# Cross-attention over 25,088 keys: stationary columns interleaved in memory, and value products of odd key tiles walked from the last column to the first

## The chip, the core and the metric

The kernel runs on one core of one Trainium2 chip. The time is device microseconds of one execution of the whole program. The kernel before takes 586.98 us (median of two runs, 586.13 and 587.82). The execution that the profiler recorded took 586.28 us.

## What is computed

One block of a perceiver: 256 latent rows `x` of width 512 attend to a context of 25,088 rows, then a causal self-attention with 16 heads and a mixture of eight small experts follow. Nearly all of the time goes into the first step, which is this part of the reference (`q` is the layer-normed `x`, `k` and `v` are the context; there is no softmax, the weights are sigmoids):

```python
qp = jnp.einsum('bsd,ed->bse', q, Wq) + bq
kp = jnp.einsum('bsd,ed->bse', k, Wk) + bk
vp = jnp.einsum('bsd,ed->bse', v, Wv) + bv
z = jnp.einsum('bqe,bke->bqk', qp, kp)
z = jax.nn.sigmoid(z / scale)
return jnp.einsum('bqk,bkd->bqd', z, vp)
```

Here `d` is 512 and `e` is 128. The kernel multiplies the sigmoids with the raw context and applies `Wv` once at the end, and adds the bias by the row sums of the sigmoids.

## The kernel before, in words

The context is cut into 49 chunks of 512 keys, and each chunk into four key tiles of 128. It comes twice, transposed (`ctxT`, for the key projection) and plain (`ctxN`, for the value product).

Every matmul operand is held as two float32r tensors, a high half that ScalarE writes (`copy`, L64) and a low half, the remainder, that VectorE writes (L65). A product is then three matmuls, high x high, high x low, low x high, in `mm3` (L67 to L70). In a matmul the stationary operand (`lhsT`, 128 columns) is loaded into the array first, and the moving operand (`rhs`) then streams past it; each moving column gives one output column in PSUM.

Per chunk `c` of the loop (L263 and on), the engines get:

- `kp_mm(c + 1)`, the key projection: stationary `wk` (four blocks of 128 columns, high and low in two tiles of 512), moving `T`, 512 columns: 4 x 3 matmuls into the bank `kp_ps`. `kp_out` adds the bias (ScalarE L178, VectorE L179) and makes `kp`.
- `av(c, t, q)`, the value product, for key tile `t` (0 to 3) and half `q` (0 or 1) of the 256 latent rows: stationary `z`, the 128 sigmoids of that tile and half, moving `N`, the 512 context columns, accumulated over the whole loop into `acc0` and `acc1`: 8 x 3 matmuls.
- `scores(c + 1, p)` for the pairs of key tiles `p` = 0 (tiles 0 and 1) and `p` = 1 (tiles 2 and 3): stationary `kp`, moving `qp`, 256 columns: 2 x 2 x 3 matmuls into `sc`. The sigmoid (ScalarE L187) gives `z` in float32, VectorE adds it to the running row sums `zacc` (L189), and `split` makes the high and low tiles of the pair, 512 columns each: columns of tile 0 and then of tile 1, and within a tile rows 0 to 127 and then 128 to 255.
- the splits of the next chunks' `T` and `N` (2048 columns each), and, spread over the loop, the preparing of later weights (`prepare`).

`z` has four buffers for each half and pair, `T`'s high half and `N` have two, `T`'s low half has one. In the last two chunks `av` runs for `q` = 0 alone, and the rest is used later as filler (`AV1`). `in_order` keeps each engine's instructions in the order in which the program was written; Tile adds the semaphores. All loads are issued from SP's queue in the order of the code.

Before the loop, `wk` is loaded and split once, the high half by ScalarE, the low half by GpSimd. At the end, in the experts, the tiles `fr` and `fq` (the gated products) lie where `wk`'s two tiles were.

Of the kernel before, what the change touches and what calls it, by code (L numbers as in the profile page):

```python
# [11 lines left out]
F32 = mybir.dt.float32  # L12
F32R = mybir.dt.float32r
# [7 lines left out]
P = 128  # L21
T = 256
D = 512
KD = D // P
# [3 lines left out]
NT = CK // P  # L28
E = 8
NH = 16  # L30
LAG = 2
# [17 lines left out]
def body(ctx, tc, a, out, nch=NCH):  # L49
    nc = tc.nc  # L50
# [4 lines left out]
    sb = ctx.enter_context(tc.tile_pool(name="sb", bufs=1))  # L55
# [3 lines left out]
    def f(t):  # L59
        return t.bitcast(F32)  # L60

    def split(hi, lo, src, eng=nc.vector):

        copy(hi, src)  # L64
        eng.tensor_tensor(lo, src, f(hi), ALU.subtract)  # L65

    def mm3(ps, ahi, alo, bhi, blo, first, last):  # L67
        mm(ps, lhsT=ahi, rhs=bhi, start=first, stop=False)  # L68
        mm(ps, lhsT=ahi, rhs=blo, start=False, stop=False)  # L69
        mm(ps, lhsT=alo, rhs=bhi, start=False, stop=last)  # L70

    def pair(name, shape, tag=None, bufs=1):
        return [sb.tile(shape, F32R, tag=f"{tag or name}{i}", name=f"{name}_{i}", bufs=bufs) for i in range(2)]

    def bank(name):
        return psum.tile([P, D], F32, tag="b", name=name, bufs=6)
# [4 lines left out]
    def toks(t):  # L81
        return slice(t * P, (t + 1) * P)
# [39 lines left out]
    def moments(x, tag):  # L122
        s6 = sm.tile([P, nc.vector.BN_STATS_DIM], F32, tag="s6", name=f"s6{tag}", bufs=2)
        mv = sm.tile([P, 2], F32, tag="mv", name=f"mv{tag}", bufs=2)
        rs = sm.tile([P, 1], F32, tag="rs", name=f"rs{tag}", bufs=2)
        nc.vector.bn_stats(s6, x)
        nc.vector.bn_aggr(mv, s6)
        nc.vector.tensor_scalar(rs, mv[:, 1:2], 1e-5, None, ALU.add)
        nc.gpsimd.tensor_tensor(rs, rs, half, ALU.pow)
        return mv, rs  # L130
# [12 lines left out]
    rT, rN, sT, sN, kp, zz = {}, {}, {}, {}, {}, {}  # L143
# [24 lines left out]
    def kp_mm(c, blocks=range(KD)):  # L168
        th, tl = sT[c]
        if c not in kp:  # L170
            kp[c] = bank(f"kp_ps{c}")
        ps = kp[c]
        for j in blocks:
            mm3(ps, wk[0][:, toks(j)], wk[1][:, toks(j)], th[:, j, :], tl[:, j, :], j == 0, j == KD - 1)

    def kp_out(c):
        ps, kp[c] = kp[c], pair(f"kp{c}", [P, CK], "kp", 2)
# [3 lines left out]
    def scores(c, p):  # L181
        ps = bank(f"sc{c}_{p}").rearrange("p (i t) -> p i t", i=2)
        for i in range(2):
            t = toks(2 * p + i)
            mm3(ps[:, i, :], kp[c][0][:, t], kp[c][1][:, t], qp[0], qp[1], True, True)
        z = sb.tile([P, 2, T], F32, tag="z", name=f"z{c}_{p}", bufs=2)
        nc.scalar.activation(z, ps, AF.Sigmoid, scale=1.0 / math.sqrt(128.0))  # L187
        zz[c, p] = pair(f"z{c}_{p}", [P, 2, T], "z", 2 * LAG)
        tt2(zacc, zacc, z, ALU.add)  # L189
        split(*zz[c, p], z)  # L190

    def av(c, t, q):
        zh, zl = zz[c, t // 2]
        nh, nl = sN[c]
        mm3(acc[q], zh[:, t % 2, toks(q)], zl[:, t % 2, toks(q)], nh[:, t, :], nl[:, t, :],
            c == 0 and t == 0, c == nch - 1 and t == NT - 1)

    def prepare(n):

# [12 lines left out]
    def load_split(n, tag):  # L212
        r = sb.tile([P, D], F32, tag="wr", name=f"{n}_r", bufs=2)
        nc.sync.dma_start(r, a[n])
        return r, pair(n, [P, D], tag)

    wk_r, wk = load_split("wk", "wk")
    for t in range(2):
        nc.sync.dma_start(x_sb[t], a["x"][:, t, :])
    wq_r, wq = load_split("wq", "at")  # L220
# [9 lines left out]
    acc = [psum.tile([P, D], F32, tag=f"acc{q}", name=f"acc{q}") for q in range(2)]  # L230
    xh, xl = pair("xa", [P, KD, T], "oh")
    warm = sm.tile([P, 1], F32, name="warm")
    nc.scalar.activation(warm, half, AF.Sigmoid)
    split(*wk, wk_r, nc.gpsimd)
    m = [moments(x_sb[tt], f"a{tt}") for tt in range(2)]
    xn = [normal(x_sb[tt], m[tt], f"xa{tt}") for tt in range(2)]
    split(*wq, wq_r, nc.gpsimd)
# [1 line left out]
    for j in range(2):  # L239
        split_T(0, [j])  # L240
        split(xh[:, :, toks(j)], xl[:, :, toks(j)], xps[j])
    split_T(0, [2, 3], nc.gpsimd)
    kp_mm(0, [0, 1])
    qp = pair("qp", [P, T])
    ps = bank("qp_ps")[:, :T]
    for j in range(KD):
        mm3(ps, wq[0][:, toks(j)], wq[1][:, toks(j)], xh[:, j, :], xl[:, j, :], j == 0, j == KD - 1)
    kp_mm(0, [2, 3])
    split_T(1, [0, 1])
    split_T(1, [2, 3], nc.gpsimd)  # L250
    nc.scalar.activation(qp[0], ps, AF.Identity, bias=bq)
    nc.vector.scalar_tensor_tensor(qp[1], ps, bq, f(qp[0]), ALU.add, ALU.subtract)
    kp_out(0)
    split_N(0, [0, 1])
    kp_mm(1, [0, 1])
    scores(0, 0)
    scores(0, 1)
    split_N(0, [2, 3])
    kp_mm(1, [2, 3])
# [3 lines left out]
    for c in range(nch):  # L263
# [23 lines left out]
        for t in range(NT):  # L287
            for q in now:
                av(c, t, q)
            if nx and t in (1, 2):  # L290
                scores(c + 1, t - 1)
# [265 lines left out]
    def AV1(n):  # L557
        for _ in range(min(n, len(late))):
            av(*late.pop(0), 1)
# [5 lines left out]
    ps = bank("rows_ps")  # L565
# [54 lines left out]
    Q(1, 2)  # L620
    Q(1, 3)
    ft = sb.tile([P, 2 * D], F32R, tag="wq2", name="ft").rearrange("p (n b e d) -> p n b e d", n=2, b=2, e=2)
    fr, fq = (sb.tile([P, 2, 2, P], F32, tag=f"wk{i}", name=f"f{i}") for i in range(2))
    yhl = pair("y", [P, KD, T], "oh")
    PV(0, 2)
    PV(0, 3)
# [144 lines left out]
```

## Time and profile before

| what | value |
|---|---|
| the profiled execution's time | 586.28 us |
| its span | 584.5 us |
| TensorE matmul, busy | 570.6 us, 98% |
| stationary loads, busy | 481.7 us, 82% |
| VectorE, busy | 459.7 us, 79% |
| ScalarE, busy | 395.1 us, 68% |
| value-product matmuls (`acc`) | 3 x 392, about 392 ns each in the record |
| key-projection matmuls (`kp_ps`) | 3 x 196 made (4 are missing in the trace), about 391 ns each |
| score matmuls (`sc`) | 3 x 196, about 283 ns each |
| z splits on VectorE | 98, 686 ns each |
| z casts on ScalarE | 98, 623 ns each |

A matmul's record covers its whole way through the array, so neighbouring records overlap: matmuls of 512 columns start about 0.227 us apart in the loop although each lasts 0.39. The granted TensorE clock is full over the span. Times in the timeline are microseconds from the span's start; what stands in brackets at the end of a line is the idle time before that instruction and what ended it.

### The profile page before, as it was taken

How to read it: one execution, taken by the hardware profiler on the slowest of the kernel's cores; microseconds unless marked ns; L12 is line 12 of the kernel's file. 1: busy time of each engine (PE TensorE's matmuls, PEld its weight loads, DVE VectorE, ACT ScalarE, POOL GpSimd, SP SyncE). 2: the span in 40 equal slices, each digit the busy share in tenths (PEclk: the TensorE clock that was granted, in tenths of full speed). 3: DMA queues.
4: the chain of work that ended last, by engine and by line, in shares of the span. 5: the costliest groups of instructions: out<-in, count | busy, mean ns of one | idle time of the engine just before them, and what ended most of it. 6: DMA issues, size and time to landing. Idle time of an engine off the chain costs nothing.

```text
span 584.5 us, 8061 instructions
## 1 busy us (share of the span) xinstructions
PE 570.6 (98%) x3036; PEld 481.7 (82%) x3036; DVE 459.7 (79%) x528; ACT 395.1 (68%) x512; POOL 21.1 (4%) x28
## 2 busy tenths in 40 slices
PE   4999999999999999999999999999999999999997
PEld 3888888888888888888888888888888887876996
DVE  6898888888888888888888888787878765667543
ACT  5877777777777777777777776767676752574211
POOL 5200000000000000000000000000000041000000
PEclk9999999999999999999999999999999999999999
DMA  8897887879888888788988887565657477700000
GB/s 288 334 368 283 278 295 281 321 278 317 287 324 276 325 271 325 266 337 298 332 282 319 274 337 245 208 225 206 234 198 243 149 295 262 316 1 1 1 1 36
DMA packets 33526, 144.94 MB, mean 248 GB/s; under 512 B 4240, under 2 KB 4432, under 8 KB 19792
## 3 DMA queue, kind: packets, MB, share of 16 engines
q1 hardware_dynamic: 33488, 144.44, 69.3%
q8 instruction: 23, 0.38, 0.2%
q14 instruction: 15, 0.12, 0.1%
HBM read 129.22 MB, written 15.20 MB: 247 GB/s over the span
## 4 chain that ended last, share of the span: by engine, by line
PE 95%; DVE 3%; DMA 1%; issue 0%; POOL 0%; ACT 0%; SPq 0%; POOLq 0%
PE acc L68 15%; PE acc L69 15%; PE acc L70 15%; PE kp_ps L70 8%; PE kp_ps L69 8%; PE kp_ps L68 8%; PE sc L70 4%; PE sc L69 4%; PE sc L68 4%; PE s L428 2%; PE gu L68 1%; PE gu L69 1%; PE gu L70 1%; PE pt L445 1%; DMA wq_r<-in_wq 1%; PE pv L456 1%
## 5 line engine op out<-in xcount | busy, mean ns | idle before, releaser
L68 PE MATMUL acc<-N,z 128*128 128x512 f32 x392 | 153.9, 393 | 0.0
L69 PE MATMUL acc<-N,z 128*128 128x512 f32 x392 | 153.7, 392 | 0.0
L65 DVE TENSOR_TENSOR N<-rN,N 128x2048 fp32r<-128x2048 f32 (+1 forms) x53 | 111.6, 2110 | 52.3 <-ACT N L64 52.2
L70 PE MATMUL acc<-N,z 128*128 128x512 f32 x392 | 152.5, 389 | 0.0
L65 DVE TENSOR_TENSOR T<-rT,T 128x2048 fp32r<-128x2048 f32 (+1 forms) x49 | 110.3, 2252 | 15.3 <-ACT T L64 15.3
L187 ACT ACTIVATE z<-sc 128x512 f32<-128x512 f32 x98 | 58.7, 599 | 66.5 <-PE sc L70 66.2
L64 ACT CAST N<-rN 128x2048 fp32r<-128x2048 f32 (+1 forms) x55 | 94.4, 1725 | 6.1
L64 ACT CAST T<-rT 128x2048 fp32r<-128x2048 f32 (+1 forms) x55 | 94.3, 1721 | 0.9 <-DMA rT<-in_ctxT 0.7
L70 PEld LDWEIGHTS acc<-N,z 128*128 128x128 f32 x392 | 73.6, 188 | 16.0
L68 PEld LDWEIGHTS acc<-N,z 128*128 128x128 f32 x392 | 74.0, 189 | 12.3
L69 PEld LDWEIGHTS acc<-N,z 128*128 128x128 f32 x392 | 74.0, 189 | 11.7
L68 PE MATMUL kp_ps<-T,wk 128*128 128x512 f32 x196 | 76.9, 392 | 0.0
L70 PE MATMUL kp_ps<-T,wk 128*128 128x512 f32 x196 | 76.7, 392 | 0.0
L69 PE MATMUL kp_ps<-T,wk 128*128 128x512 f32 x192 | 74.7, 389 | 0.0
L189 DVE TENSOR_TENSOR zacc<-zacc,z 128x512 f32<-128x512 f32 x98 | 67.2, 686 | 3.7 <-ACT z L187 1.7
L65 DVE TENSOR_TENSOR z<-z,z 128x512 fp32r<-128x512 f32 x98 | 67.3, 686 | 0.0
L64 ACT CAST z<-z 128x512 fp32r<-128x512 f32 x98 | 61.0, 623 | 3.1
L178 ACT ACTIVATE kp<-kp_ps,bk 128x512 fp32r<-128x512 f32 x49 | 33.9, 691 | 39.9 <-PE kp_ps L70 39.9
L70 PE MATMUL sc<-qp,kp 128*128 128x256 f32 x196 | 55.8, 285 | 0.1
L69 PE MATMUL sc<-qp,kp 128*128 128x256 f32 x196 | 55.4, 283 | 0.0
L68 PE MATMUL sc<-qp,kp 128*128 128x256 f32 x196 | 54.9, 280 | 0.0
L68 PEld LDWEIGHTS kp_ps<-T,wk 128*128 128x128 f32 x196 | 37.1, 189 | 7.8
(177 smaller groups left out, 658.5 us busy)
## 6 DMA issues: line engine op xcount, KB each, us to landing
rN<-in_ctxN SPq DMA_DIRECT2D x49, 1024.0 KB, 5.7
rT<-in_ctxT SPq DMA_DIRECT2D x47, 1024.0 KB, 5.5
sp_gu<-w_gu SPq DMA_DIRECT2D x32, 256.0 KB, 4.3
gu<-sp_gu SPq DMA_DIRECT2D x8, 1024.0 KB, 6.0
r_gu<-in_gu SPq DMA_DIRECT2D x16, 256.0 KB, 5.7
sp_dn<-w_dn SPq DMA_DIRECT2D x16, 256.0 KB, 4.3
dn<-sp_dn SPq DMA_DIRECT2D x16, 256.0 KB, 6.0
r_dn<-in_dn SPq DMA_DIRECT2D x8, 256.0 KB, 6.1
```

The lines of the kernel that those rows point to most:

```text
L64: copy(hi, src)
L65: eng.tensor_tensor(lo, src, f(hi), ALU.subtract)
L68: mm(ps, lhsT=ahi, rhs=bhi, start=first, stop=False)
L69: mm(ps, lhsT=ahi, rhs=blo, start=False, stop=False)
L70: mm(ps, lhsT=alo, rhs=bhi, start=False, stop=last)
L178: nc.scalar.activation(kp[c][0], ps, AF.Identity, bias=bk)
L187: nc.scalar.activation(z, ps, AF.Sigmoid, scale=1.0 / math.sqrt(128.0))
L189: tt2(zacc, zacc, z, ALU.add)
L428: mm(p3[:, h - h0:h - h0 + 2, :], lhsT=qs[:, tt, h // 2, g, :], rhs=kbd[g // 2][:, g % 2, h:h + 2, :nk], start=tt == 1, stop=tt == 0 and h ...
L445: nc.tensor.transpose(ps[:, toks(i * (tt + 1) + kt)], pr[tt, u][:, i, toks(kt)], ident)
L456: mm(pv[tt][r, g, :], lhsT=vs[kt][:, g * P + r.start:g * P + r.stop], rhs=pt[tt, u][:, toks(i * (tt + 1) + kt)], start=kt == 0, stop=kt == tt)
```

## The change

Three things about addresses, and no arithmetic:

- `wk` is one tile `[128, 4, 128, 2]`: high and low half of a column lie side by side. A stationary block is read with a step of two words.
- The high tile of a `z` pair, and likewise the low one, is laid out anew. In pair 0 the two row halves of a key tile alternate (`q` innermost): a stationary block is read with a step of two words. In pair 1 the four blocks, two key tiles by two halves, alternate: a step of four words. ScalarE and VectorE write these tiles with such steps; the float32 `z` that they read stays as it was.
- In `av`, key tiles 1 and 3 pass `back=True`: moving operand and output are both taken from column 511 down to 0, so each output column still gets its own sum.

`kp`, `qp`, `T` and the score matmuls stay. `fr` and `fq` become two halves of one tile at `wk`'s place.

```diff
-    def mm3(ps, ahi, alo, bhi, blo, first, last):
+    def mm3(ps, ahi, alo, bhi, blo, first, last, back=False):
+        if back:
+            ps, bhi, blo = ps[:, ::-1], bhi[:, ::-1], blo[:, ::-1]
         mm(ps, lhsT=ahi, rhs=bhi, start=first, stop=False)
...
-            mm3(ps, wk[0][:, toks(j)], wk[1][:, toks(j)], th[:, j, :], tl[:, j, :], j == 0, j == KD - 1)
+            mm3(ps, wk[:, j, :, 0], wk[:, j, :, 1], th[:, j, :], tl[:, j, :], j == 0, j == KD - 1)
...
-        zz[c, p] = pair(f"z{c}_{p}", [P, 2, T], "z", 2 * LAG)
+
+        if p == 0:
+            zz[c, p] = [t.rearrange("p (i t q) -> p i q t", i=2, q=2) for t in pair(f"z{c}_{p}", [P, 2 * T], "z", 2 * LAG)]
+        else:
+            zz[c, p] = [t.rearrange("p (t i q) -> p i q t", i=2, q=2) for t in pair(f"z{c}_{p}", [P, 2 * T], "z", 2 * LAG)]
         tt2(zacc, zacc, z, ALU.add)
-        split(*zz[c, p], z)
+        split(*zz[c, p], z.rearrange("p i (q t) -> p i q t", q=2))
...
-        mm3(acc[q], zh[:, t % 2, toks(q)], zl[:, t % 2, toks(q)], nh[:, t, :], nl[:, t, :],
-            c == 0 and t == 0, c == nch - 1 and t == NT - 1)
+        mm3(acc[q], zh[:, t % 2, q], zl[:, t % 2, q], nh[:, t, :], nl[:, t, :],
+            c == 0 and t == 0, c == nch - 1 and t == NT - 1, t % 2 == 1)
...
-    wk_r, wk = load_split("wk", "wk")
+    wk_r = sb.tile([P, D], F32, tag="wr", name="wk_r", bufs=2)
+    nc.sync.dma_start(wk_r, a["wk"])
+
+    wk = sb.tile([P, KD, P, 2], F32R, tag="wk", name="wk")
...
-    split(*wk, wk_r, nc.gpsimd)
+    split(wk[:, :, :, 0], wk[:, :, :, 1], wk_r.rearrange("p (j c) -> p j c", j=KD), nc.gpsimd)
...
-    fr, fq = (sb.tile([P, 2, 2, P], F32, tag=f"wk{i}", name=f"f{i}") for i in range(2))
+    frq = sb.tile([P, 2, 2, 2, P], F32, tag="wk", name="frq")
+    fr, fq = frq[:, 0], frq[:, 1]
```

## The prediction

> **What bounds the kernel now.** I read the page's first part, its chain and its groups, then the timeline of TensorE in three places and that of VectorE over one chunk. First the page: span and busy time, the chain by engine, and the groups that the change touches.
>
> ```profile
> span 584.5 us, 8061 instructions
> ...
> PE 570.6 (98%) x3036; PEld 481.7 (82%) x3036; DVE 459.7 (79%) x528; ACT 395.1 (68%) x512; POOL 21.1 (4%) x28
> ...
> PE 95%; DVE 3%; DMA 1%; issue 0%; POOL 0%; ACT 0%; SPq 0%; POOLq 0%
> ...
> L68 PE MATMUL acc<-N,z 128*128 128x512 f32 x392 | 153.9, 393 | 0.0
> ...
> L65 DVE TENSOR_TENSOR N<-rN,N 128x2048 fp32r<-128x2048 f32 (+1 forms) x53 | 111.6, 2110 | 52.3 <-ACT N L64 52.2
> ...
> L70 PEld LDWEIGHTS acc<-N,z 128*128 128x128 f32 x392 | 73.6, 188 | 16.0
> ...
> L65 DVE TENSOR_TENSOR z<-z,z 128x512 fp32r<-128x512 f32 x98 | 67.3, 686 | 0.0
> ...
> L64 ACT CAST z<-z 128x512 fp32r<-128x512 f32 x98 | 61.0, 623 | 3.1
> ```
>
> TensorE carries 95% of the chain and has no idle time ahead of its large groups, so the end moves with the time from one matmul's start to the next. That is not the 393 ns of the row, which overlaps with its neighbours; it has to be read from starts. Timeline of TensorE in the steady loop (start, duration, engine, line, operands):
>
> ```profile
> 199.99 0.28 PE L68 MATMUL sc<-qp,kp 128*128 128x256 f32 x1
> 200.11 0.28 PE L69 MATMUL sc<-qp,kp 128*128 128x256 f32 x1
> ...
> 201.74 0.39 PE L68 MATMUL kp_ps<-T,wk 128*128 128x512 f32 x1
> ...
> 204.46 0.39 PE L68 MATMUL acc<-N,z 128*128 128x512 f32 x1
> ```
>
> Twelve key projections start between 201.74 and 204.46: 2.72 / 12 = 0.2267 us each. Score matmuls, half as wide, start 0.120 apart. The same key projections near the beginning of the run, before TensorE is at full speed:
>
> ```profile
> 11.76 0.63 PE L68 MATMUL kp_ps<-T,wk 128*128 128x512 f32 x1
> 12.19 0.63 PE L69 MATMUL kp_ps<-N,wk 128*128 128x512 f32 x1
> 12.61 0.63 PE L70 MATMUL kp_ps<-T,wk 128*128 128x512 f32 x1
> ```
>
> There they start 0.427 apart. Half of that is 0.2133, and 0.2267 is 13.3 ns more. For the 256-wide ones 0.120 is also about 13 ns more than 512 : 256 of 0.2133. So each full-speed matmul carries a fixed 13.3 ns that doesn't depend on its width; as each has one stationary load, I put it down to that load. This is the term on which the change acts.
>
> A chunk is 36 matmuls of 512 columns and 12 of 256: 36 x 0.2267 + 12 x 0.120 = 9.60 us. VectorE's timeline shows the same period and its slack:
>
> ```profile
> 300.29 2.29 DVE L65 TENSOR_TENSOR N<-rN,N 128x2048 fp32r<-128x2048 f32 x1 [1.12 <-ACT N L64]
> ...
> 304.10 2.29 DVE L65 TENSOR_TENSOR T<-rT,T 128x2048 fp32r<-128x2048 f32 x1 [0.26 <-ACT T L64]
> 306.31 0.68 DVE L189 TENSOR_TENSOR zacc<-zacc,z 128x512 f32<-128x512 f32 x1
> 306.91 0.68 DVE L65 TENSOR_TENSOR z<-z,z 128x512 fp32r<-128x512 f32 x1
> 307.51 0.68 DVE L189 TENSOR_TENSOR zacc<-zacc,z 128x512 f32<-128x512 f32 x1
> ...
> 309.93 2.29 DVE L65 TENSOR_TENSOR N<-rN,N 128x2048 fp32r<-128x2048 f32 x1 [1.13 <-ACT N L64]
> ```
>
> The period is 309.93 - 300.29 = 9.64 us, of which VectorE is idle 1.12 + 0.26 = 1.38 us.
>
> **What the Trainium skill says.** "TensorE: Matmul & The Clock Gate", Step-by-step: what each phase is for, states that moving operand and stationary load have separate read ports, so that a load takes nothing from the running matmul; the 13.3 ns above speak against "nothing" in this kernel. "SBUF — State Buffer", Specifications, gives 16-byte lines and asks for at least two hits per line for full rate: a step of two fp32 words still has two, a step of four has one. "PSUM — Partial Sum Buffer", Specifications, has 8-byte lines and says that non-contiguous patterns slow matmuls; whether a backward walk over neighbours counts as that, it doesn't say. "Vector Engine (DVE) Microarchitecture Reference", Measured stream behaviour on trn2, gives 1.05 ns per column for neighbours and 1.7 to 2.5 ns when a stream steps over words. No access of the kernel before has an inner step other than 1 word on these operands, so its trace confirms none of the last three.
>
> **The change part by part.** The order of instructions on every engine is the same, and so is the count. What moves is addresses.
>
> 1. Key projection: 49 chunks x 12 = 588 loads read wk with a step of 2 words. Unknown on the trace. Bounds per matmul: -13.3 ns (the fixed part goes) to +13.3 ns (twice as many lines, twice the fixed part). Value: 0.
> 2. Value products of the first pair of key tiles: 49 x 12 = 588 loads, step 2. The same bounds and value.
> 3. Value products of the second pair: 588 loads, step 4. From -13.3 to +40 ns (four times the lines). A load occupies at most 0.120 us, because score matmuls bring one each in that time; if one hit per line makes it twice as long, 0.240 is 13 ns over the 0.2267 that cover it, which is within the bounds. Value: 0. I take 0 in all three because the timeline has the same 0.2267 for key projections and for the first pair's value products, and 0.228 to 0.236 for those right after scores (200.35, 200.59, 200.82), whatever tiles they read; that is what a cost of the load itself would do, whatever it reads.
> 4. Backward walk in odd tiles: 49 x 2 tiles x 2 x 3 = 588 matmuls read N and write acc from the last column to the first. Neighbours stay neighbours, in both memories. From 0 to +0.200 us each (the rate of the slow stage, 0.427 in place of 0.2267). Value: 0.
> 5. VectorE's z splits: two per chunk, 0.60 us from start to start (306.91 to 307.51), now with an input and the output at step 2 or 4. By the skill's prices, estimate: 512 x (1.7 to 2.5) + the 0.06 that 0.60 has over 512 x 1.05 = 0.93 to 1.34 us, so 0.33 to 0.74 more each, 0.66 to 1.48 per chunk. The cover is the 1.38 us of idle time; the high end passes it by 0.1 us x 48 chunks = 5 us. Late next would be the N split behind it, then kp's low half, on which the third score matmul waits. Value: 0.
> 6. ScalarE's z casts write with the same steps; no row prices it. Doubling them (+0.62 each) fits in the waits of the z and kp activations for TensorE, 66.2 + 39.9 us over 49 chunks, or 2.2 per chunk, though the N cast then starts later and eats of point 5's cover. A gain is worth nothing here. Value: 0.
> 7. wk's split happens once: ScalarE 0.62 us and GpSimd 1.26 us, ending near 5.3 us, long before the first key projection at 10.3 us. Only the GpSimd operation of the layer norm that follows at 5.34 could be pushed; x's second half isn't there until 6.03, so half a microsecond is covered. Value +0.3 us at most. The shared tile of the gated products at the end keeps its addresses and waits.
>
> Sum: 586.3 (the profiled execution: span 584.5 and 1.8 around it) + 0.3 = 586.6 us. The median of the runs is 0.7 above that execution, so 587.3 us.
>
> **The rivals.**
>
> - *More lines per load cost more (slower).* The place is the 13.3 ns. For: it is there only at full speed, as if two streams contended for memory, and 13.3 ns for 32 lines of 512 bytes would be one short beat a line. Against: "separate ports". If each of 1764 loads pays it twice: 1764 x 13.3 ns = +23.5 us, 610 us. If it goes by lines: 1176 x 13.3 + 588 x 40 ns = 15.6 + 23.5 = +39.1 us, 626 us. I take 611. It decides from 11.7 us on, 6.7 ns per load.
> - *The backward walk is slow.* For: the PSUM page. Against: the pairs stay pairs. In full, 588 x 0.200 = +118 us, 705 us; with half of it 646. I take 700.
> - *The fixed part shrinks (faster).* If load and stream contend because both climb at a fixed pace from equally aligned tiles, other steps or directions could part them. In full, 1764 x 13.3 = -23.5 us: 563 us. Half of it: 575. Nothing in the trace shows it, but nothing excludes it.
> - *VectorE becomes the bound.* From 0.69 us more per z split on. At 3 ns per column (prices that add): (1.60 - 1.29) x 2 x 48 = +30 us, 617; nearer the threshold 594. I take 600.
>
> **How the numbers follow.** Unchanged 0.32 (own range 584 to 592), more lines 0.24, shrinking 0.25, backward slow 0.14, VectorE 0.05. 2% of 587 is 11.7 us, about what a measurement of this kernel can tell from no change, so the marks are 575 and 599. Faster: half of the shrinking case, 0.13. Slower: 0.21 of more lines, 0.13 of backward, 0.03 of VectorE: 0.37. Within 2%: 0.50. The range 568 to 640 leaves out about 0.07 below and 0.11 above.
>
> **What would show it.** Right: starts of kp_ps and acc matmuls 0.2267 apart in all four key tiles, chunks of 9.64 us, z splits longer on VectorE and its idle time shorter. If kp_ps is at 0.240 and the second pair near 0.267, lines count; if tiles 1 and 3 differ from 0 and 2, it is the walk; at 0.213 to 0.220 the contention went; if kp's low half or N's split releases TensorE with its starts unchanged, it is VectorE.

## The result, and the profile after

The changed kernel takes 609.0 us (median of two runs, 608.47 and 609.52), the kernel before 586.98 us: a ratio of 1.0375, 95% interval 1.030 to 1.045. It is slower by 22 us. That lies inside the stated range (568 to 640), but not where the likeliest case put it (587.3); it is near the size that the first rival gave (611).

The page of the kernel after, the same parts as those shown of before:

```profile
span 607.5 us, 8061 instructions
...
PE 592.3 (97%) x3036; PEld 523.6 (86%) x3036; DVE 486.1 (80%) x528; ACT 415.2 (68%) x512; POOL 21.6 (4%) x28
...
PE 94%; DVE 3%; ACT 1%; POOL 1%; issue 0%; DMA 0%; POOLq 0%
...
L70 PE MATMUL acc<-N,z 128*128 128x512 f32 x392 | 167.1, 426 | 0.0
...
L71 PE MATMUL acc<-N,z 128*128 128x512 f32 x392 | 155.4, 397 | 0.0
...
L72 PEld LDWEIGHTS acc<-N,z 128*128 128x128 f32 x392 | 99.1, 253 | 8.3 <-DVE z L65 0.6
...
L65 DVE TENSOR_TENSOR z<-z,z 128x512 fp32r<-128x512 f32 x98 | 89.5, 913 | 21.5 <-ACT z L64 21.5
...
L64 ACT CAST z<-z 128x512 fp32r<-128x512 f32 x98 | 89.7, 915 | 3.1
```

TensorE still makes up the chain and still has next to no idle time ahead of the value products. Their loads waited for `z` once in the whole run, 0.6 us in the last chunk (the L72 line), so in the loop's steady chunks nothing new releases TensorE. But the records of the stationary loads for `acc` went from 188 to 253 ns in the mean, which mixes the loads of step 2 and of step 4. And of the three matmul lines the first grew by 33 ns (393 to 426), the other two by 5 to 8 (L71 to 397). One line out of three means that a place in the sequence is hit, besides something small that all share. The timeline of TensorE and its loads before, where a block of scores ends and value products begin:

```profile
200.24 0.19 PEld L68 LDWEIGHTS acc<-N,z 128*128 128x128 f32 x1
...
200.35 0.40 PE L68 MATMUL acc<-N,z 128*128 128x512 f32 x1
200.35 0.19 PEld L69 LDWEIGHTS acc<-N,z 128*128 128x128 f32 x1
...
200.59 0.40 PE L69 MATMUL acc<-N,z 128*128 128x512 f32 x1
```

Each load starts together with a matmul and belongs to the next one. The same place after, then the end of the last key tile's value products and the key projections:

```profile
199.50 0.28 PE L72 MATMUL sc<-qp,kp 128*128 128x256 f32 x1
199.50 0.31 PEld L70 LDWEIGHTS acc<-N,z 128*128 128x128 f32 x1
199.62 0.51 PE L70 MATMUL acc<-N,z 128*128 128x512 f32 x1
199.72 0.33 PEld L71 LDWEIGHTS acc<-N,z 128*128 128x128 f32 x1
199.97 0.40 PE L71 MATMUL acc<-N,z 128*128 128x512 f32 x1
...
201.13 0.40 PE L70 MATMUL kp_ps<-T,wk 128*128 128x512 f32 x1
201.13 0.20 PEld L71 LDWEIGHTS kp_ps<-T,wk 128*128 128x128 f32 x1
...
203.93 0.39 PE L70 MATMUL acc<-N,z 128*128 128x512 f32 x1
```

Two things are to be seen. First, the load that starts with the last score matmul at 199.50 is still going on when the first value product is due at 199.62. That matmul's record is 0.51 us long in place of 0.40; I read the 0.11 more as its wait for the load. The next load starts only at 199.72, 0.22 after the first, and its matmul at 199.97, 0.35 us after its predecessor, where 0.233 was usual. Second, the twelve key projections from 201.13 to 203.93 are (203.93 - 201.13) / 12 = 0.2333 us apart, 6.7 ns more than before.

Times from a matmul's start to the next one's start, means over the 46 equal chunks of the loop, in ns:

| place in the chunk | before | after |
|---|---|---|
| key projection, 12 | 226.7 | 233.3 |
| value products tile 0, 6 | 226.7 | 233.3 |
| value products tile 1 (backward), 6 | 226.7 | 234.9 |
| scores, 12 | 118.9 | 118.8 |
| tile 2, first matmul after scores | 233.0 | 355.0 |
| tile 2, the other five | 230.9 | 234.7 |
| tile 3 (backward), first matmul after scores | 233.1 | 344.2 |
| tile 3, the other five | 230.8 | 233.3 |
| whole chunk | 9641 | 10073 |

A chunk is 432 ns longer. The two gaps after scores are (355.0 - 233.0) + (344.2 - 233.1) = 233 ns of that, the other 199 ns are spread over the matmuls of 512 columns ("wide" from here on). Of the 23.0 us by which the span grew, the 46 chunks make 46 x 0.432 = 19.9; the time up to the loop's second chunk 1.7, the last chunk 1.2 (there VectorE's low half of z is late, 0.6 us), the rest 0.2.

VectorE over one chunk:

```profile
300.65 0.68 DVE L65 TENSOR_TENSOR z<-z,z 128x512 fp32r<-128x512 f32 x1
...
302.38 1.14 DVE L65 TENSOR_TENSOR z<-z,z 128x512 fp32r<-128x512 f32 x1 [0.44 <-ACT z L64]
304.10 2.29 DVE L65 TENSOR_TENSOR N<-rN,N 128x2048 fp32r<-128x2048 f32 x1 [0.58 <-ACT N L64]
```

The split at step 2 takes 0.68 us as before, the one at step 4 takes 1.14. VectorE waits for ScalarE afterwards (0.58 us), so in the loop the longer split is covered.

### The profile page after: what moved, and what is told of

It reads as the page before. It is cut to its first block, busy times and chain, and to the rows that moved or that the text cites. A ratio compares the mean times of both kernels' runs of the same rounds, so it can differ in the third digit from the quotient of the medians.

```text
span 607.5 us, 8061 instructions
## 1 busy us (share of the span) xinstructions
PE 592.3 (97%) x3036; PEld 523.6 (86%) x3036; DVE 486.1 (80%) x528; ACT 415.2 (68%) x512; POOL 21.6 (4%) x28
## 4 chain that ended last, share of the span: by engine, by line
PE 94%; DVE 3%; ACT 1%; POOL 1%; issue 0%; DMA 0%; POOLq 0%
PE acc L70 16%; PE acc L72 15%; PE acc L71 15%; PE kp_ps L72 8%; PE kp_ps L71 8%; PE kp_ps L70 7%; PE sc L72 4%; PE sc L71 4%; PE sc L70 4%; PE s L437 2%; PE gu L70 1%; PE gu L71 1%; PE gu L72 1%; PE pt L454 1%; PE pv L465 1%; PE fo L70 1%
## 5 line engine op out<-in xcount | busy, mean ns | idle before, releaser
L70 PE MATMUL acc<-N,z 128*128 128x512 f32 x392 | 167.1, 426 | 0.0
L72 PE MATMUL acc<-N,z 128*128 128x512 f32 x392 | 155.7, 397 | 0.3 <-DVE z L65 0.3
L71 PE MATMUL acc<-N,z 128*128 128x512 f32 x392 | 155.4, 397 | 0.0
L71 PEld LDWEIGHTS acc<-N,z 128*128 128x128 f32 x392 | 101.3, 258 | 7.7
L65 DVE TENSOR_TENSOR z<-z,z 128x512 fp32r<-128x512 f32 x98 | 89.5, 913 | 21.5 <-ACT z L64 21.5
L72 PEld LDWEIGHTS acc<-N,z 128*128 128x128 f32 x392 | 99.1, 253 | 8.3 <-DVE z L65 0.6
L70 PEld LDWEIGHTS acc<-N,z 128*128 128x128 f32 x392 | 98.8, 252 | 7.8
L64 ACT CAST z<-z 128x512 fp32r<-128x512 f32 x98 | 89.7, 915 | 3.1
L70 PE MATMUL kp_ps<-T,wk 128*128 128x512 f32 x196 | 77.9, 397 | 0.0
L72 PE MATMUL kp_ps<-T,wk 128*128 128x512 f32 x196 | 77.7, 396 | 0.0
L71 PE MATMUL kp_ps<-T,wk 128*128 128x512 f32 x192 | 75.6, 394 | 0.0
L72 PE MATMUL sc<-qp,kp 128*128 128x256 f32 x196 | 55.5, 283 | 0.9 <-DVE kp L181 0.9
L71 PE MATMUL sc<-qp,kp 128*128 128x256 f32 x196 | 55.2, 282 | 0.0
L72 PEld LDWEIGHTS kp_ps<-T,wk 128*128 128x128 f32 x196 | 38.1, 194 | 7.7
```

## The experiments

My theory after the result: the loss lies in the stationary loads. A load with a step of 2 words costs 6.7 ns per wide matmul, a step of 4 makes the load itself about twice as long, which is uncovered only right after scores. The rivals were that the backward walk costs, that z is finished late, and that the writes of z disturb all matmuls. Each ratio below is against runs of the kernel before on the same chip (585.98 to 586.46 us). A run of one execution has no interval; its trace still averages over 46 chunks.

### One part alone

**e1_back_only** puts the backward walk into the kernel before:

```diff
-    def mm3(ps, ahi, alo, bhi, blo, first, last):
+    def mm3(ps, ahi, alo, bhi, blo, first, last, back=False):
+        if back:
+            ps, bhi, blo = ps[:, ::-1], bhi[:, ::-1], blo[:, ::-1]
...
-            c == 0 and t == 0, c == nch - 1 and t == NT - 1)
+            c == 0 and t == 0, c == nch - 1 and t == NT - 1, t % 2 == 1)
```

> Before, with the backward walk of key tiles 1 and 3 alone; all stationary operands as before. Theory 'loads' (the loss lies in the stationary loads, the walk is free but for single steps of 3 to 7 ns where the direction turns): value products stay 0.2267 us apart in all tiles, time 587 to 588 us. Rival 'walk' (backward reading or writing costs part of it): tiles 1 and 3 slower than 0 and 2 by 6.7 ns or more in each matmul, +4 us or more, 591 us or more.

Measured: 589.4 us, ratio 1.0051 (1.0033 to 1.0069). The first value product of tile 1 in its timeline, and the score matmul that follows the sixth:

```profile
206.41 0.40 PE L70 MATMUL acc<-N,z 128*128 128x512 f32 x1
...
207.81 0.28 PE L70 MATMUL sc<-qp,kp 128*128 128x256 f32 x1
```

That is (207.81 - 206.41) / 6 = 0.233 us each. The means are 234.0 ns in tile 1 against 226.7 before, and 233.3 against 230.8 for the last five of tile 3. The time lies between the two expectations. But the walk is not free: with step-1 loads it costs tile 1 some 7 ns per matmul, as much as a step of 2, and "the walk is free" falls.

**e2_wk_only** interleaves `wk` alone (the four edits of the change that name `wk`).

> Before, with wk's high and low half interleaved (step 2) and nothing else. Theory 'loads': key projections go from 0.2267 to 0.2333 us from start to start, 588 x 6.7 ns = +3.9 us, 591 us; value products stay at 0.2267. Rival 'traffic' (the 6.7 ns come from the spaced writes of z on ScalarE and VectorE, which disturb every matmul): key projections stay at 0.2267, 587 us.

Measured: 590.4 us, 1.0061 (1.0044 to 1.0078). Key projections are 233.3 ns apart, value products 226.7 to 227.3 in tiles 0 and 1. The step of the load in question is enough, without any spaced write of z; "traffic" isn't needed for the 6.7 ns. e3_z2_only, next, has the other half: with the spaced writes of z and `wk` as before, the key projections stand at 227.3.

**e3_z2_only** has step 2 in both z pairs:

```diff
-        zz[c, p] = pair(f"z{c}_{p}", [P, 2, T], "z", 2 * LAG)
+        zz[c, p] = [t.rearrange("p (i t q) -> p i q t", i=2, q=2) for t in pair(f"z{c}_{p}", [P, 2 * T], "z", 2 * LAG)]
...
```

> Before, with both z pairs at step 2, no step 4, no backward walk, wk as before. Theory 'loads': value products at 0.2333 us, 1176 x 6.7 ns = +7.8 us, 595 us, and no long gap at the first value product after scores (0.24 at most). Rival 'z late' (the gaps of 0.355 and 0.344 us come from z being finished late by the spaced writes): gaps there of 0.3 us or more, 600 us or more. Rival 'walk': the 6.7 ns do not appear, 587 us.

Measured: 591.4 us, 1.0086 (1.0067 to 1.0105). Value products are 233.2 to 233.3 ns apart, and the first after scores 230.0: no gap. The total is 3.6 us under my number, for the most part because tiles 2 and 3 had stood at 230.8 to 233 before already, so they lose little.

**e13_z4p1** has step 4 in pair 1 alone:

```diff
-        zz[c, p] = pair(f"z{c}_{p}", [P, 2, T], "z", 2 * LAG)
+        zz[c, p] = [t.rearrange(f"p ({'t i q' if p else 'i q t'}) -> p i q t", i=2, q=2) for t in pair(f"z{c}_{p}", [P, 2 * T], "z", 2 * LAG)]
...
```

> Before, with step 4 for z of pair 1 alone; pair 0, wk and the walk as before. Theory 'uncovered loads': only the first value product after each block of scores grows, from 0.233 to about 0.35 us, twice in a chunk, 49 x 0.23 = 11 us, and a few ns on the others of pair 1; 597 to 601 us. Rival: the gap needs wk's step or the walk as well; under 593 us.

Measured: 602.4 us, 1.0272 (1.0252 to 1.0292), a little over the expected range.

```profile
204.85 0.51 PE L68 MATMUL acc<-N,z 128*128 128x512 f32 x1
205.20 0.40 PE L69 MATMUL acc<-N,z 128*128 128x512 f32 x1
```

The gaps are there, 345.2 and 346.6 ns in the mean, without `wk`'s step or the walk. The chunk is 302 ns longer: 226 in the two gaps, and the rest spread, some 38 of it over the key projections, whose operands are as before. Why those lose time too isn't shown. This part by itself makes most of the loss.

### Is it the load or a late z?

**e4_swap** exchanges the layouts of the two pairs in the kernel after:

```diff
-        if p == 0:
+        if p == 1:
```

> The kernel after with the layouts of the two pairs exchanged: pair 0 has step 4, pair 1 step 2. The number of step 4 loads, the slow z split and the slow z cast stay the same. Theory 'loads' (a step 4 load lasts 0.31 us and is uncovered only where it must fit behind a 256-column score matmul): pair 0's tiles follow key projections and tile 0, so no gap is left; all 36 wide matmuls at 0.233, chunks of 9.84 us, 49 x 0.23 = 11 us less than after, 598 us. Rival 'z late': the gaps move to tile 0 or stay, 607 to 611 us.

Measured: 597.7 us, 1.0186 (1.0168 to 1.0204), 11.3 us less than after. Its timeline, first from the key projections into tile 0 (step 4), then from scores into tile 2 (step 2):

```profile
208.87 0.40 PE L72 MATMUL kp_ps<-T,wk 128*128 128x512 f32 x1
209.11 0.40 PE L70 MATMUL acc<-N,z 128*128 128x512 f32 x1
209.34 0.40 PE L71 MATMUL acc<-N,z 128*128 128x512 f32 x1
```

```profile
202.69 0.28 PE L72 MATMUL sc<-qp,kp 128*128 128x256 f32 x1
202.81 0.39 PE L70 MATMUL acc<-N,z 128*128 128x512 f32 x1
203.04 0.40 PE L71 MATMUL acc<-N,z 128*128 128x512 f32 x1
```

There is no gap in either. As many loads have step 4 as in the kernel after, and as many splits and casts are slow; what runs ahead of those loads differs. And in none of the 46 chunks, here or in the kernel after, does a load wait for z. So the gap is a load that the matmul ahead of it doesn't cover, and "z late" is out. The covered step-4 loads cost a little more than step 2: 235.1 and 235.8 ns in tiles 0 and 1.

**e5_all2** is the kernel after with pair 1 at step 2 too.

> The kernel after with pair 1 at step 2 as well, so that no load has step 4; wk at step 2 and the backward walk stay. Theory 'loads and direction': all wide matmuls at 0.2333 us, no gap over 0.24 at the first value product after scores, z splits 0.69 us and z casts 0.68 us; the parts don't add where tiles 1 and 3 have both step and walk; 596 us. Rival 'parts add' (walk and step each cost 6.7 ns also together): tiles 1 and 3 at 0.240, 598 us or more.

Measured: 594.6 us, 1.0143 (1.0126 to 1.016). Key projections and tile 0 are at 233.3 ns, tile 1, where the direction turns, at 234.9, and tiles 2 and 3 at 229 to 233; there is no gap. The parts don't add: a backward matmul with a step-2 load has 233.3 in the steady stretch, as with either alone, and the 8.3 us lost in all are no more than the 4.0 and 4.9 of e2_wk_only and e3_z2_only together. Against the kernel after, step 4 in pair 1 is worth 609.0 - 594.6 = 14.4 us.

### The load by itself

Score matmuls have 256 columns and start 0.120 us apart, each with a load of its own. A load that takes longer than that must show there, so `kp` is the place to time it.

**e10_kp4** stores `kp`'s four key tiles by turns:

```diff
+        ps = ps.rearrange("p (u t c) -> p u t c", u=1, t=4)
+        kp[c] = [k.rearrange("p (u c t) -> p u t c", u=1, t=4) for k in kp[c]]
...
-            t = toks(2 * p + i)
-            mm3(ps[:, i, :], kp[c][0][:, t], kp[c][1][:, t], qp[0], qp[1], True, True)
+            u, t = divmod(2 * p + i, 4)
+            mm3(ps[:, i, :], kp[c][0][:, u, t], kp[c][1][:, u, t], qp[0], qp[1], True, True)
```

> Before, with kp's four key tiles by turns (step 4), the stationary operand of the score matmuls; wk, z and the walk as before. [...] Theory 'a step 4 load takes twice the time': score matmuls start 0.23 to 0.24 us apart in place of 0.120, 588 x 0.115 = +68 us, about 650 us, and load records of 0.31 us. Rival 'z late': the load of a step of 4 costs what others cost, scores stay at 0.12 to 0.13, under 600 us.

Measured: 643.9 us in one run. Its timeline:

```profile
200.35 0.39 PE L69 MATMUL sc<-qp,kp 128*128 128x256 f32 x1
200.58 0.39 PE L70 MATMUL sc<-qp,kp 128*128 128x256 f32 x1
200.82 0.39 PE L68 MATMUL sc<-qp,kp 128*128 128x256 f32 x1
201.05 0.39 PE L69 MATMUL sc<-qp,kp 128*128 128x256 f32 x1
```

Score matmuls whose load starts with a score matmul are 0.2333 us apart, where they were 0.120. That is the pace of a step-4 load, and the number that explains the gaps: it passes a score matmul by 0.113, and the gaps are 0.111 to 0.122. A wide matmul's 0.2267 it passes by only 0.007.

**e8_kp2** interleaves `kp`'s high and low half (step 2).

> Before, with kp's high and low half by turns (step 2), so that the score matmuls[...] load with step 2. Theory 'two words of a line keep the load's pace': scores stay 0.117 to 0.121 us apart, 586 to 589 us. Rival 'every step costs the load time': scores at 0.127 us or more, 590 us or more.

Measured: 586.6 us in one run; scores 118.7 ns apart in the mean, 118.9 before, and a chunk of 9641 ns, as before. A step-2 load still fits into a score matmul's time, at most 0.119 us, although its record is 195 ns long in place of 190. Whether it is slower than a step-1 load within that time isn't shown. What it costs a wide matmul is therefore not the load's length.

**e9_step8** lets pair 1's high and low halves alternate too, eight blocks by turns.

> The kernel after with pair 1 at step 8: high and low half by turns too, eight blocks. Theory 'lines' (one memory line a column from step 4 on, and no more than one): load records 0.31 us, gaps of 0.35 us after scores, 607 to 611 us as the kernel after. Rival 'distance' (the load's time grows with the step): load records of 0.4 us or more, 615 us or more.

Measured: 614.8 us in one run. Gaps of 362 and 355 ns, and 245 to 248 ns for the other matmuls of tiles 2 and 3; load records up to 0.349 us. Neither side is right: from 4 to 8 words the time between wide matmuls grows by 5 to 6%, not to twice and not by nothing.

### What are the 6.7 ns?

**e6_step0** loads one column 128 times in the value products, so it leaves out the other 127 and its sums are not those of the value product; it serves the timing alone:

```diff
-        mm3(acc[q], zh[:, t % 2, toks(q)], zl[:, t % 2, toks(q)], nh[:, t, :], nl[:, t, :],
+        mm3(acc[q], *(x[:, t % 2, q * P:q * P + 1].broadcast_to([P, P]) for x in (zh, zl)), nh[:, t, :], nl[:, t, :],
```

> Before, but each value product loads the first column of its z block 128 times (step 0), so the value products are computed with the wrong weights; nothing else changes. Theory 'lines' (the 13.3 ns that a matmul takes beyond half of its slow-stage time come from the memory lines that the load reads beside the stream): value products start less than 0.2267 us apart, down to 0.2133. Rival 'fixed' (13.3 ns belong to a load whatever it reads): 0.2267 stays.

Measured: 590.4 us in one run. Value products are 234, 233 and 226 ns apart by turns in tiles 0 and 1, mean 231. Both theories fail: with the fewest possible lines the cost went up, and it isn't fixed.

**e12_zshift** starts each z tile 32 bytes further:

```diff
-        zz[c, p] = pair(f"z{c}_{p}", [P, 2, T], "z", 2 * LAG)
+        zz[c, p] = [t[:, 8:2 * T + 8].rearrange("p (i t) -> p i t", i=2) for t in pair(f"z{c}_{p}", [P, 2 * T + 16], "z", 2 * LAG)]
```

> Before, with each z tile starting 32 bytes later within its 64 bytes; steps and walk as before. Theory 'phase' (load and stream disturb each other by where in memory they are at one moment): value products leave 0.2267 us, up or down by a multiple of some ns; 583 to 592 us, not equal to before. Rival 'addresses don't matter, only step and direction do': 0.2267 stays, 586 to 587 us.

Measured: 591.0 us, 1.0079 (1.0062 to 1.0095). Value products stand at 231 to 236 ns in tiles 0 and 1. With step, direction and number of columns unchanged, a shift in address costs 5 us, within what theory 'phase' allowed. (The tiles are 64 bytes longer for it, so what is placed behind them can move too; no run parts the two.)

**e11_sc_back** walks the score matmuls alone backward.

> Before, with the score matmuls alone walking backward over qp and their output. Theory 'direction of load and stream matters wherever both run': scores change from 0.120, to 0.127 us if the load suffers as the stream does (588 x 6.7 ns = +4 us, 590 us). Rival 'load-bound matmuls don't see the stream's direction': 0.120 stays, 586 to 587 us.

Measured: 584.6 us, 0.9978 (0.9965 to 0.9991). It is 0.2% faster, against my theory and below the rival's 586: scores 118.0 ns in the mean, and the value products after them recover sooner (227.5 in place of 230.9 after the first). This is the one version that beats the kernel before, by 1.4 us.

So the small term is shown to depend on the step of the load, the direction of the stream and the address of the stationary tile: each moves the wide matmuls between 226.7 and about 236 ns. By what mechanism stays open. The count of lines doesn't explain it, and a forward walk is the better one for wide matmuls with step-1 loads but not for scores.

## Why the prediction was right and wrong

**Bound and method: right.** TensorE bounds both kernels, time moved with start-to-start spacing, and in the 46 chunks no other engine took over.

**The sum: wrong, and the range right by its width.** The sum (587.3 us) had neither of the terms that made the loss: some 46 x 0.233 = 10.7 us in the gaps and 46 x 0.199 = 9.2 us spread over the wide matmuls. That 609 lies between 568 and 640 is owed to the room left for the rivals.

**Step 3 is the one that failed.** It said of a load at step 4 that twice 0.120 would be 0.240, "13 ns over the 0.2267 that cover it". The doubling was right: 0.2333, against at most 0.120 (e10_kp4, e8_kp2). The cover was wrong. Two of the eight groups of three value-product loads in a chunk begin behind a score matmul, which covers 0.120 and not 0.2267. I looked up the cover in the steady row and didn't ask what runs ahead of the first load of each block. From its own numbers the step should have had 2 x (0.240 - 0.120) x 49 = +11.8 us; the trace shows 2 gaps of 0.111 to 0.122 in each chunk. Its 13 ns over the cover, on 588 loads, would have been another 7.8 us, and were put at 0 as well; the other matmuls of tiles 2 and 3 in fact grew by 2.5 to 3.8 ns.

**Steps 1 and 2 were mis-sized:** value 0, measured +6.7 ns on 12 key projections and 12 value products, 0.17 us in a chunk, near 8 us in all. It was inside the bounds. My reason for 0, that the 13.3 ns belong to the load whatever it reads, is refuted by e2_wk_only, e6_step0 and e12_zshift: the spacing moves with what is read. That the whole excess is 13.3 ns rests on taking half of the 0.427 at the start of the run, where the profile grants the same clock (1.00) as later; 0.2267 and 0.120 at two widths fit it, and no run tests it.

**Step 4:** value 0, and in the kernel after near to that by luck, not for the reason given (no run takes the walk alone out of the kernel after; e5_all2 and the sum of the parts say so). Alone the walk costs 0.5%; on top of step-2 loads only the turns show (235.8 and 240.0 ns at tile 1's first and last matmul). The full price, a rate as in the slow stage, does not occur.

**Steps 5 and 6:** hidden in the 46 chunks, as said. The prices that the prediction took from the Trainium skill, "Vector Engine (DVE) Microarchitecture Reference", Measured stream behaviour on trn2, fit at step 4 only: (1.14 - 0.68) / 512 = 0.9 ns more per column on VectorE, within the 0.65 to 1.45 that the page's 1.05 and 1.7 to 2.5 give as an estimate. At step 2 the split took 0.68 us as before; there the measurement decides. ScalarE's cast took 1.16 us in place of 0.62. In the last chunk, where only one half of the value products is left as cover, the late z cost 0.6 us of TensorE's time.

**The rivals:** "more lines" named the right sign and, by luck, a near total (611), with the wrong make-up: neither 13.3 ns per load nor lines as the cause of the small term, and no gaps. "Shrinking" did not come true in this change; e11_sc_back shows that a little of it exists. The split of chances left 0.37 for slower, and the arithmetic of step 3 spoke for more.

**Start of the loop:** +0.3 us was expected at most for `wk`'s split; 0.3 came there, and 1.4 more up to the loop's second chunk. Most of that is one place: the third score matmul of the first chunk waits 0.93 us for `kp`'s low half, which VectorE makes behind the longer z split, which in turn waits for ScalarE's longer cast. It is the wait that step 5 named and put at 0; in the 46 equal chunks it does not come.

## What to carry to other kernels

In these traces a stationary load is hidden only by the matmul directly ahead of it, so when loads may get longer, check the cover at each seam where a narrow matmul precedes a wide one, not the average. Expect about half the load's pace at a step of 4 fp32 words; at 2 the load still fitted into 0.119 us, though wide matmuls went from 0.2267 to 0.2333. This agrees with the Trainium skill, "SBUF — State Buffer", Specifications, which asks for at least two hits per 16-byte line for full bandwidth: a step of 2 has two, a step of 4 one. That step 8 cost some 5% more isn't explained by it. If matmuls are bound by start-to-start spacing, try start address and direction of both operands one at a time: they moved a wide matmul by 2 to 4% here, and the sign wasn't known beforehand.

## What the runs showed of the hardware that was not expected

- A step-4 load has a pace of 0.2333 us for 128 columns, a step-1 or step-2 load at most 0.120. At step 8 the wide matmuls behind which such loads run are 245 to 248 ns apart, some 5% over that pace.
- Reading one column 128 times is not the cheapest load: 231 ns per wide matmul, against 226.7 with 128 neighbouring columns.
- Starting z 32 bytes later, in tiles 64 bytes longer, costs 0.8%, and turning the direction of the score matmuls gains 0.2%, with the same instructions in the same order.
- Walking the moving operand and the output backward costs a wide matmul with step-1 loads some 7 ns in the steady stretches and nothing measurable on top of step-2 loads (0.2333 us), far from half its rate.
